# A row-wise tail written out by hand: the last twelve rows of a triangle-multiplication and gated-pair kernel

## The chip, the cores and the metric

The kernel runs on one core of one Trainium2 chip. A core has five engines with instruction queues of their own: TensorE (PE in the profile; its weight loads are PEld), VectorE (DVE), ScalarE (ACT), GpSimd (POOL) and SyncE (SP), which here only issues DMA transfers. Each engine works its queue off in order; an instruction that waits holds up everything behind it. SBUF is the on-chip memory, PSUM the small memory that TensorE writes to and that VectorE and ScalarE can read and write. The metric is the device time of the whole kernel in microseconds (us), as a median over runs.

## The reference

The input is one map x of 384 x 384 positions with 128 channels, in float32. Two layers follow one another.

```
layer 0:  z_n = layernorm(z)                                 # over channels
          a = (z_n Wa + ba) * sigmoid(z_n Wga + bga);  b likewise
          X[i,k,d] = sum_j a[i,j,d] * b[j,k,d]               # per channel a 384x384 product
          pair = z + (layernorm(X) Wo + bo) * sigmoid(z_n Wgo + bgo)
layer 1:  left  = pair W_left + b_left + pair W_eq + b_eq
          gate  = sigmoid(pair W_gate + b_gate)
          right_sum[i] = sum over k of (pair W_right + b_right)
          out   = (left * right_sum * gate) W_out + b_out
          y     = layernorm(out + pair) * ln_scale + ln_bias
```

The last line matters most here: every position's 128 channels get a mean and a variance, are normalised by them, and then scaled and shifted with one value per channel.

## The kernel before

The kernel has three phases. Phase 1 (lines 100 to 388) normalises x, makes the gated factors a and b, and writes them to DRAM with the gate and the residual. Phase 2 (lines 450 to 547) makes the 128 channels' products and their statistics. Phase 3 (lines 552 to 688) finishes layer 0 and does all of layer 1, row by row: row u is one i with its 384 positions, laid out as three pieces (NB = 3) of 128 positions on the 128 partitions, each piece with 128 channels. Rows are loaded and finished in groups of R = 4.

Phase 3 is one software pipeline: the loop over u at line 682 runs through a list of stages, and each stage works on row u minus a lag. The order in which the code names the instructions is the order of every engine's queue. The stages, by function:

- `layer_0` (line 595): three products give the layer-0 output of row u in PSUM; VectorE scales and gates it (L608) and adds the residual (L615) to make `pair`. The same function takes the statistics (L613, L618) of `res` of row u - 8.
- `turn` (line 562): three transposes of `pair` into the PSUM tile `ptr`, of which there is one; ScalarE copies it out to `pairT` and adds up the row for `right_sum` (L568).
- `project` (line 640): the left product (PSUM tile `pleft`, two buffers) and the gate product (PSUM tile `pg`, one buffer); ScalarE's sigmoid (L650). For the first row of a group the right product of the group before is put into the same `pg` bank (L656) and taken out by L652.
- `gate_product` (line 577): VectorE multiplies left and gate to `h` (L580).
- `out_weights` (line 571): ScalarE scales W_out by the row's right sum (L574).
- `layer_1` (line 583): three products of `h` and those weights into the PSUM tile `pf` (two buffers); VectorE adds `pair` and writes `res` to SBUF (L593).
- `norm_factors` (line 620): once per group, on GpSimd: variance plus epsilon, the power -1/2 (L626), mean times that, negated (L625 to L629).
- `normalise` (line 632): ScalarE, in place on `res`, three instructions a row (L635), each with a scale and a bias per partition.
- `store` (line 664): for most groups GpSimd multiplies four rows at once by ln_scale (L674) and adds ln_bias (L675), then SP issues one store of 768 KB (L676). For the last eight rows VectorE does it row by row (L668, L669), with a store of 192 KB each (L670).
- `last_right` (line 658): the right product of the last group.

The loop runs on for 17 steps after the last row has come in, in which fewer and fewer stages have work. In those steps the products, the statistics, the factors and the scaling of rows 372 to 383 follow the same lags as in the loop.

Of the kernel before, what the change touches and what calls it, by code (L numbers as in the profile page):

```python
# [8 lines left out]
FP = mybir.dt.float32  # L9
AF = mybir.ActivationFunctionType  # L10
ALU = mybir.AluOpType
# [4 lines left out]
EPS = 1e-5  # L16
# [3 lines left out]
def kernel(ctx: ExitStack, tc: tile.TileContext, ins, out: bass.AP):  # L20
# [15 lines left out]
    nc = tc.nc  # L36
    ctx.enter_context(tc.manual_schedule())
    P = 128
    x = ins["x"][0]
    N, C = x.shape[1], x.shape[2]  # L40
    NB = N // P
    y_out = out[0]
# [10 lines left out]
    def ctile(shape, name):  # L53
        return const.tile(shape, FP, tag=name, name=name)

    ident = ctile([P, P], "ident")
# [5 lines left out]
    def column(name, q=None):  # L62
        t = ctile([P, 1], "c_" + name)
        (q or nc.sync).dma_start(out=t, in_=ins[name].rearrange("(c o) -> c o", o=1))
        return t

    def rows(name, q=None):
        t = ctile([P, C], "r_" + name)
        (q or nc.sync).dma_start(out=t, in_=ins[name].partition_broadcast(P))
        return t  # L70

    def matrix(name):
        t = ctile([P, P], "m_" + name)
        nc.sync.dma_start(out=t, in_=ins[name])
        return t
# [6 lines left out]
    def over(t, n):  # L82
        return t[:, None, :].to_broadcast([P, n, C])
# [19 lines left out]
    with tc.tile_pool(name="wprep", bufs=6) as wp, tc.tile_pool(name="p1s", bufs=3) as ps, tc.tile_pool(  # L103
        name="p1g", bufs=2
    ) as pgt, tc.tile_pool(name="p1x", bufs=4) as px, tc.tile_pool(name="p1a", bufs=2) as pa_, tc.tile_pool(
        name="p1b", bufs=1, side="right"
    ) as pb_, tc.tile_pool(name="p1t", bufs=2, space=PSUM) as ppt, tc.tile_pool(
        name="p1p", bufs=6, space=PSUM
# [237 lines left out]
        for _ in x_parts:  # L346
# [7 lines left out]
        w_left, w_eq, w_right, w_gate, w_out = (  # L354
            matrix(L1 + k) for k in ("W_left", "W_eq", "W_right", "W_gate", "W_out")
        )
        b_left, b_eq, b_right, b_gate = (column(L1 + k) for k in ("b_left", "b_eq", "b_right", "b_gate"))
        ln_s, ln_b = rows(L1 + "ln_scale"), rows(L1 + "ln_bias")
# [41 lines left out]
    LAST, AHEAD, R, HELD = 8, 6, 4, 16  # L400
    group = {}
# [44 lines left out]
    def advance(g, n=1):  # L446
        for _ in range(n):
            next(g, None)

    with tc.tile_pool(name="p2", bufs=1, side="right", reuse_waits="tile") as p2, tc.tile_pool(  # L450
        name="p2s", bufs=12, side="right", reuse_waits="tile"
    ) as p2s, tc.tile_pool(name="p2p", bufs=5, space=PSUM, reuse_waits="tile") as pp2, tc.tile_pool(
        name="p2q", bufs=2, space=PSUM, reuse_waits="tile"
# [98 lines left out]
    with tc.tile_pool(name="p3s", bufs=4, reuse_waits="tile") as ps, tc.tile_pool(  # L552
        name="p3g", bufs=4, reuse_waits="tile"
    ) as pg3, tc.tile_pool(name="p3y", bufs=2, space=PSUM, reuse_waits="tile") as pyp, tc.tile_pool(
        name="p3p", bufs=1, space=PSUM, reuse_waits="tile"
    ) as pp:
        pairs, hs, wos = {}, {}, {}

        def of(u):
            return group[u // R], u % R  # L560
# [94 lines left out]
        def right(g, pg):  # L655
            nc.tensor.matmul(pg[:, N : N + R], lhsT=w_right, rhs=g["total"], start=True, stop=True)  # L656

        def last_right(u):
            if u == N:
                g, pg = group[N // R - 1], pp.tile([P, 512], FP, tag="pg", name="pg_last")  # L660
                right(g, pg)
                nc.scalar.activation(g["right"], pg[:, N : N + R], AF.Identity, bias=b_right)

        def store(u):
            if u >= N - 2 * R:
                g, i = of(u)
                res = g["res"][:, i]
                nc.vector.tensor_tensor(res, res, over(ln_s, NB), ALU.mult)  # L668
                nc.vector.tensor_tensor(res, res, over(ln_b, NB), ALU.add)  # L669
                nc.sync.dma_start(out=y_out[u].rearrange("(p q) c -> p q c", q=NB), in_=res)  # L670
            elif u % R == 0:
                g = group.pop(u // R)
                res = g["res"].rearrange("p r q c -> p (r q) c")
                nc.gpsimd.tensor_tensor(res, res, over(ln_s, R * NB), ALU.mult)  # L674
                nc.gpsimd.tensor_tensor(res, res, over(ln_b, R * NB), ALU.add)  # L675
                nc.sync.dma_start(out=y_out[u : u + R].rearrange("i (p q) c -> p i q c", q=NB), in_=g["res"])  # L676

        stages = (
            (load, -2 * R), (gate_product, 3), (turn, 2), (out_weights, 7), (layer_1, 8), (layer_0, 0),
            (norm_factors, 12), (normalise, 13), (project, 2), (last_right, 2), (store, 17),  # L680
        )
        for u in range(N + stages[-1][1]):
            for stage, lag in stages:
                if stage is layer_0:
                    stage(u, u - 8)
                elif 0 <= u - lag < N or (stage is last_right and u - lag == N):
                    stage(u - lag)
            advance(behind)


_INS = ["x"] + [
# [33 lines left out]
```

## Time and profile before

| what | us |
|---|---|
| median of three runs | 3340.28 (3338.49 to 3342.46) |
| the profiled execution's own time | 3343.24 |
| its span in the trace | 3341.5 |
| TensorE busy | 3293.7 |
| VectorE busy | 2666.1 |
| ScalarE busy | 2311.3 |
| GpSimd busy | 2091.9 |
| one row in the steady loop of phase 3 (start to start of a row's L593) | 3.0 |
| last row's layer-0 products start | 3304.0 |
| last product of the kernel starts (L592) | 3322.8 |
| VectorE's last instruction ends (L669) | 3338.3 |

The span runs from the first to the last record of one execution; the execution's own time is a little longer. A duration of an instruction is from its start to its end; the next one on the same engine can start up to about 0.1 us before that end, so the distance from start to start is what adds up. "Idle before" names the wait that ended last before an instruction.

### The profile page before, as it was taken

What the parts mean: (1) busy time and instruction counts of PE and PEld (TensorE: products, weight loads), DVE (VectorE), ACT (ScalarE), POOL (GpSimd) and SP (SyncE); (2) the same over time, 40 slices, a digit from 0 to 9 for tenths busy, and PEclk for the clock granted to TensorE, in tenths of its full rate; (3) what the DMA queues carried; (4) which work ended last, traced back from release to release, by engine and by line L of the source; (5) the groups of instructions that cost most, each with busy time, mean ns of one, the idle gap of its engine ahead of it and who ended that gap; (6) DMA issues with size and microseconds to landing.
All of it is one profiled execution on the core that took longest, in us unless ns stands there. A gap on an engine that the chain in (4) does not pass through costs nothing.

```text
span 3341.5 us, 53397 instructions
## 1 busy us (share of the span) xinstructions
PE 3293.7 (99%) x15581; PEld 2191.3 (66%) x15581; DVE 2666.1 (80%) x8599; ACT 2311.3 (69%) x5488; POOL 2091.9 (63%) x1574
## 2 busy tenths in 40 slices
PE   8999999999999999999999999999999999999997
PEld 5555555555555555555555555588888888888885
DVE  8877777777777777455555555799999999999998
ACT  7778787877777788522222222378888888888887
POOL 7555555555555555355555555358888888888887
PEclk9999999999999999999999999999999999999998
DMA  6889899889888889899999999767777777777774
GB/s 226 265 256 273 278 282 282 278 279 281 280 269 264 268 275 282 254 337 318 312 315 311 312 311 304 258 231 262 261 263 262 262 262 264 264 263 263 263 265 142
DMA packets 675522, 910.52 MB, mean 272 GB/s; under 512 B 319520, under 2 KB 616480, under 8 KB 647712
## 3 DMA queue, kind: packets, MB, share of 16 engines
q1 hardware_dynamic: 634192, 680.28, 63.9%
q0 software_dynamic: 40320, 226.51, 19.3%
q8 instruction: 126, 2.06, 0.2%
q14 instruction: 164, 1.34, 0.1%
q10 hardware_dynamic: 720, 0.33, 0.0%
HBM read 454.04 MB, written 452.98 MB: 271 GB/s over the span
## 4 chain that ended last, share of the span: by engine, by line
PE 96%; DVE 2%; POOL 1%; DMA 1%; ACT 0%; issue 0%; POOLq 0%; ACTq 0%; SPq 0%; DVEq 0%
PE pm L488 22%; PE pga L246 8%; PE pa L246 7%; PE pgb L246 7%; PE pb L246 7%; PE py L602 7%; PE pf L592 7%; PE pgo L211 7%; PE pleft L643 7%; PE pg L645 7%; PE ptr L180 4%; PE ptr L566 4%; DMA G<-gt 0%; DVE py L608 0%; PE pg L656 0%
## 5 line engine op out<-in xcount | busy, mean ns | idle before, releaser
L488 PE MATMUL pm<-ab 128*128 128x384 f32 x2304 | 746.6, 487 | 5.8 <-DVE gs L213 5.8
L488 PEld LDWEIGHTS pm<-ab 128*128 128x128 f32 x2304 | 438.9, 191 | 312.4 <-DVE gs L213 6.7
L507 POOL TENSOR_TENSOR acc<-acc,xd 128x384 f32<-128x384 f32 x381 | 380.1, 998 | 362.4 <-DVE xd L500 362.2
L505 ACT ACTIVATE sq<-xd 128x384 f32<-128x384 f32 x381 | 188.5, 495 | 542.3 <-DVE xd L500 542.2
L276 DVE SCALAR_TENSOR_TENSOR bt<-pb,c_L_conv_bb,sgb 128x512 f32<-128x512 f32 x288 | 320.9, 1114 | 243.3 <-ACT zT L191 218.6
L160 ACT ACTIVATE zn<-xt,off,rstd 128x128 f32<-128x128 f32 x1152 | 503.3, 489 | 2.9 <-POOL off L151 2.8
L635 ACT ACTIVATE res<-res,off,rs 128x128 f32<-128x128 f32 x1152 | 482.5, 486 | 18.4 <-POOL off L629 15.7
L500 DVE TENSOR_TENSOR xd<-pm,acc 128x384 f32<-128x384 f32 x381 | 212.2, 557 | 343.3 <-POOL acc L507 321.3
L608 DVE SCALAR_TENSOR_TENSOR py<-py,acc,gr 128x128 f32<-128x128 f32 x1152 | 433.7, 377 | 2.2 <-PE py L602 1.6
L267 POOL DMA_DIRECT2D A<-at x72 | 85.4, 1186 | 539.2 <-DVE at L263 539.2
L251 ACT ACTIVATE sga<-pga,c_L_conv_bga 128x512 f32<-128x512 f32 x288 | 197.9, 687 | 267.6 <-PE pga L246 267.6
L211 PEld LDWEIGHTS pgo<-wT_go,zT 128*128 128x128 f32 x2176 | 285.7, 192 | 130.0 <-issue 66.5
L613 DVE BATCH_NORM_STATS2 st<-res 128x6 f32<-128x128 f32 x1152 | 361.4, 315 | 0.3
L675 POOL TENSOR_TENSOR res<-res,r_L_conv_ln_bias 128x1536 f32<-128x1536 f32 x94 | 324.6, 3453 | 7.4
L171 POOL TENSOR_TENSOR acc<-xt,r_L_conv_b_out 128x2048 f32<-128x2048 f32 x72 | 327.4, 4548 | 1.8
L592 PE MATMUL pf<-w_o,h 128*128 128x128 f32 x2304 | 321.2, 276 | 6.1 <-ACT w_o L574 5.3
L674 POOL TENSOR_TENSOR res<-res,r_L_conv_ln_scale 128x1536 f32<-128x1536 f32 x94 | 325.3, 3461 | 0.2 <-issue 0.2
L650 ACT ACTIVATE sg<-pg,c_L_conv_b_gate 128x384 f32<-128x384 f32 x384 | 223.0, 581 | 144.5 <-PE pg L645 92.6
L602 PE MATMUL py<-w_o,xr 128*128 128x128 f32 x2304 | 321.1, 276 | 0.0
L643 PE MATMUL pleft<-pairT,m_L_conv_W_left 128*128 128x384 f32 x768 | 313.1, 489 | 2.8 <-ACT pairT L568 2.8
L645 PE MATMUL pg<-pairT,m_L_conv_W_gate 128*128 128x384 f32 x768 | 311.1, 487 | 0.0
L141 DVE BATCH_NORM_STATS2 st<-xt 128x6 f32<-128x128 f32 x1152 | 305.5, 265 | 3.7 <-DMA xt<-in_x_dram 3.6
(142 smaller groups left out, 6826.8 us busy)
## 6 DMA issues: line engine op xcount, KB each, us to landing
A<-at POOLq DMA_DIRECT2D x72, 1024.0 KB, 8.5
Z<-acc POOLq DMA_DIRECT2D x72, 1024.0 KB, 8.2
G<-gt POOLq DMA_DIRECT2D x72, 1024.0 KB, 9.2
xr<-X SPq DMA_DIRECT2D x96, 768.0 KB, 6.0
gr<-G SPq DMA_DIRECT2D x96, 768.0 KB, 7.6
zr<-Z SPq DMA_DIRECT2D x96, 768.0 KB, 8.8
X<-xd SPq DMA_DIRECT2D x381, 192.0 KB, 6.2
xt<-in_x_dram SPq DMA_DIRECT2D x71, 1024.0 KB, 17.9
```

Of the source, the lines that this page charges most:

```text
L160: nc.scalar.activation(g["zn"][:, c, :], g["x"][:, c, :], AF.Identity, bias=g["off"][:, c : c + 1], scale=g["rstd"][:, c : c + 1],)
L211: nc.tensor.matmul(pgo[:, c, :], lhsT=zT[:, c, :], rhs=wT["go"], start=True, stop=True)
L246: nc.tensor.matmul(pk, lhsT=wT[k], rhs=zT, start=True, stop=True)
L488: nc.tensor.matmul(products[d, ib], lhsT=ab[:, 0, q, ib * P : (ib + 1) * P], rhs=ab[:, 1, q, :], start=(q == 0), stop=(q == NB - 1),)
L507: nc.gpsimd.tensor_tensor(s1[:, ib, :], s1[:, ib, :], xd, ALU.add)
L592: nc.tensor.matmul(pf[:, q, :], lhsT=h[:, q * P : (q + 1) * P], rhs=w_o, start=True, stop=True)
L602: nc.tensor.matmul(py[:, q, :], lhsT=g["x"][:, i, q * P : (q + 1) * P], rhs=w_o0, start=True, stop=True)
L608: nc.vector.scalar_tensor_tensor(py[:, q, :], py[:, q, :], rs0[:, q, u : u + 1], g["g"][:, i, q, :], ALU.mult, ALU.mult)
L613: nc.vector.bn_stats(b["st"][:, k, q, :], b["res"][:, k, q, :])
L635: nc.scalar.activation(g["res"][:, i, q, :], g["res"][:, i, q, :], AF.Identity, bias=g["off"][:, i, q : q + 1], scale=g["rs"][:, i, q : q ...
L643: nc.tensor.matmul(pleft, lhsT=w_left, rhs=pairT, start=True, stop=True)
L645: nc.tensor.matmul(pg[:, 0:N], lhsT=w_gate, rhs=pairT, start=True, stop=True)
```

## The change

The loop now stops when the last row has come in (u = 383). What was left to the 17 further steps is written out by hand, with D = 384 as the row count. `store` always works on GpSimd and takes the number of rows as an argument. `last_right` is gone; the right product of the last group goes into a bank of the `ptr` tag. Five new functions come in:

- `layer_1_summed`: for rows 382 and 383 the residual is added by TensorE, as a product with the identity into the same bank; there is no VectorE addition, and the sum stays in PSUM.
- `statistics`: the L613 and L618 of a row, by themselves, reading PSUM for those two rows.
- `last_factors`: for the last two groups (376 to 379, 380 to 383) VectorE and ScalarE make the factors instead of GpSimd: ScalarE takes the square root of the variance, VectorE its reciprocal and one Newton step. Each VectorE instruction has at most one tensor operand in SBUF; the rest lies in PSUM, for which two results are copied out to SBUF.
- `normalise_on_gpsimd`: row 376 is normalised by GpSimd with three instructions.
- `normalise_to_bank` and `scale_and_shift`: rows 377 to 383 are normalised by ScalarE into a PSUM bank (the `pleft`, `pf` and `py` tags are used again), and VectorE multiplies in PSUM, adds and writes to SBUF; one store per row.

Rows 372 to 375 keep the factors from GpSimd and are scaled by GpSimd in two halves; row 376 is scaled by GpSimd alone.

```diff
+        def store(u, n=R):
+            if u % n:
+                return
+            g, i = of(u)
+            res = g["res"][:, i : i + n]
+            flat = res.rearrange("p r q c -> p (r q) c")
+            nc.gpsimd.tensor_tensor(flat, flat, over(ln_s, n * NB), ALU.mult)
+            nc.gpsimd.tensor_tensor(flat, flat, over(ln_b, n * NB), ALU.add)
+            nc.sync.dma_start(out=y_out[u : u + n].rearrange("i (p q) c -> p i q c", q=NB), in_=res)
...
-        for u in range(N + stages[-1][1]):
+        for u in range(N):
...
+        def bank(u):
+            tag = {7: "pleft", 6: "pleft", 5: "pleft", 4: "pf", 3: "pf", 2: "py", 1: "py"}[D - u]
+            banks[u] = pyp.tile([P, NB, C], FP, tag=tag, name=f"end_{u}")
+            return banks[u]
+
+        def layer_1_summed(u):
+            pf = bank(u)
+            h, w_o, pair = hs.pop(u), wos.pop(u), pairs.pop(u)
+            for q in range(NB):
+                nc.tensor.matmul(pf[:, q, :], lhsT=ident, rhs=pair[:, q, :], start=True, stop=False)
+                nc.tensor.matmul(pf[:, q, :], lhsT=h[:, q * P : (q + 1) * P], rhs=w_o, start=False, stop=True)
...
+        def last_factors(u):
+            g, _ = of(u)
+            few = pp.tile([P, 4, R, NB], FP, tag="ptr", name=f"few_{u}")
+            v, r, t, rs = (few[:, k] for k in range(4))
+            sd, r_, t_, rs_, off = (
+                pg3.tile([P, R, NB], FP, tag="e" + k, name=f"{k}_{u}", bufs=2) for k in ("sd", "r", "t", "rs", "off")
+            )
+            nc.vector.tensor_scalar(v, g["mv"][:, :, :, 1], EPS, None, ALU.add)
+            nc.scalar.activation(sd, v, AF.Sqrt)
+            yield
+            nc.vector.reciprocal(r, sd)
+            nc.vector.tensor_copy(r_, r)
+            nc.vector.scalar_tensor_tensor(t_, r_, -0.5, r, ALU.mult, ALU.mult)
+            nc.vector.tensor_tensor(t, t_, v, ALU.mult)
+            nc.vector.scalar_tensor_tensor(rs, t, 1.5, r_, ALU.add, ALU.mult)
+            nc.vector.tensor_copy(rs_, rs)
+            nc.vector.scalar_tensor_tensor(off, g["mv"][:, :, :, 0], -1.0, rs, ALU.mult, ALU.mult)
+            g["rs"], g["off"] = rs_, off
+
+        def normalise_on_gpsimd(u):
+            g, i = of(u)
+            for q in range(NB):
+                nc.gpsimd.tensor_scalar(
+                    g["res"][:, i, q, :], g["res"][:, i, q, :], g["rs"][:, i, q : q + 1], g["off"][:, i, q : q + 1],
+                    ALU.mult, ALU.add,
+                )
...
+        def scale_and_shift(u):
+            g, i = of(u)
+            res = g["res"][:, i]
+            nc.vector.tensor_tensor(banks[u], banks[u], over(ln_s, NB), ALU.mult)
+            nc.vector.tensor_tensor(res, banks[u], over(ln_b, NB), ALU.add)
+            nc.sync.dma_start(out=y_out[u].rearrange("(p q) c -> p q c", q=NB), in_=res)
+
+        norm_factors(D - 12)
+        turn(D - 2)
+        gate_product(D - 3)
+        out_weights(D - 7)
+        layer_1(D - 8)
+        statistics(D - 8)
+        turn(D - 1)
+        out_weights(D - 6)
+        project(D - 2)
+        normalise(D - 13)
+        store(D - 16)
+        layer_1(D - 7)
+        statistics(D - 7)
+        gate_product(D - 2)
+        out_weights(D - 5)
...
+        nc.tensor.matmul(pr[:, 0:R], lhsT=w_right, rhs=g["total"], start=True, stop=True)
+        nc.scalar.activation(g["right"], pr[:, 0:R], AF.Identity, bias=b_right)
+        layer_1(D - 6)
+        statistics(D - 6)
+        layer_1(D - 5)
+        out_weights(D - 4)
+        project(D - 1)
+        for u in range(D - 3, D):
+            out_weights(u)
+        statistics(D - 5)
+        gate_product(D - 1)
+        normalise(D - 12)
+        normalise(D - 11)
+        store(D - 12, 2)
+        first = last_factors(D - 8)
+        advance(first)
+        layer_1(D - 4)
+        statistics(D - 4)
+        layer_1(D - 3)
+        advance(first)
+        statistics(D - 3)
+        normalise(D - 10)
+        normalise(D - 9)
+        store(D - 10, 2)
+        layer_1_summed(D - 2)
+        statistics(D - 2)
+        layer_1_summed(D - 1)
+        statistics(D - 1)
+        normalise_to_bank(D - 7)
+        second = last_factors(D - R)
+        advance(second)
+        normalise_on_gpsimd(D - 8)
+        store(D - 8, 1)
+        scale_and_shift(D - 7)
+        advance(second)
+        normalise_to_bank(D - 6)
+        scale_and_shift(D - 6)
+        normalise_to_bank(D - 5)
+        scale_and_shift(D - 5)
+        for u in range(D - R, D):
+            normalise_to_bank(u)
+            scale_and_shift(u)
```

More of the change, by code (lines that the diff above doesn't have):

```diff
@@ L656, in right @@
             nc.tensor.matmul(pg[:, N : N + R], lhsT=w_right, rhs=g["total"], start=True, stop=True)
[L658 to L676, printed above, removed]
+        def store(u, n=R):
[7 more added lines that the diff above has]
+            nc.sync.dma_start(out=y_out[u : u + n].rearrange("i (p q) c -> p i q c", q=NB), in_=res)
         stages = (
             (load, -2 * R), (gate_product, 3), (turn, 2), (out_weights, 7), (layer_1, 8), (layer_0, 0),
-            (norm_factors, 12), (normalise, 13), (project, 2), (last_right, 2), (store, 17),
+            (norm_factors, 12), (normalise, 13), (project, 2), (store, 17),
         )
-        for u in range(N + stages[-1][1]):
+        for u in range(N):
             for stage, lag in stages:
@@ L685 @@
                     stage(u, u - 8)
-                elif 0 <= u - lag < N or (stage is last_right and u - lag == N):
+                elif 0 <= u - lag < N:
                     stage(u - lag)
             advance(behind)
+        D = N
+        banks = {}
+        def bank(u):
[8 more added lines that the diff above has]
+                nc.tensor.matmul(pf[:, q, :], lhsT=h[:, q * P : (q + 1) * P], rhs=w_o, start=False, stop=True)
@@ new lines, in statistics @@
+        def statistics(u):
+            g, i = of(u)
+            for q in range(NB):
+                nc.vector.bn_stats(g["st"][:, i, q, :], banks[u][:, q, :] if u in banks else g["res"][:, i, q, :])
+            for q in range(NB):
+                nc.vector.bn_aggr(g["mv"][:, i, q, :], g["st"][:, i, q, :])
+        def last_factors(u):
[16 more added lines that the diff above has]
+            g["rs"], g["off"] = rs_, off
@@ new lines, in normalise_on_gpsimd, with normalise_to_bank @@
+        def normalise_on_gpsimd(u):
+            g, i = of(u)
+            for q in range(NB):
+                nc.gpsimd.tensor_scalar(
+                    g["res"][:, i, q, :], g["res"][:, i, q, :], g["rs"][:, i, q : q + 1], g["off"][:, i, q : q + 1],
+                    ALU.mult, ALU.add,
+                )
+        def normalise_to_bank(u):
+            g, i = of(u)
+            if u in banks:
+                source = banks[u]
+            else:
+                source = g["res"][:, i]
+                bank(u)
+            for q in range(NB):
+                nc.scalar.activation(
+                    banks[u][:, q, :], source[:, q, :], AF.Identity,
+                    bias=g["off"][:, i, q : q + 1], scale=g["rs"][:, i, q : q + 1],
+                )
@@ new lines, in scale_and_shift @@
+        def scale_and_shift(u):
+            g, i = of(u)
+            res = g["res"][:, i]
[8 more added lines that the diff above has]
+        statistics(D - 8)
@@ new lines @@
+        turn(D - 1)
[7 more added lines that the diff above has]
+        out_weights(D - 5)
+        g = group[D // R - 1]
+        pr = pp.tile([P, N], FP, tag="ptr", name="pr_last")
+        nc.tensor.matmul(pr[:, 0:R], lhsT=w_right, rhs=g["total"], start=True, stop=True)
+        nc.scalar.activation(g["right"], pr[:, 0:R], AF.Identity, bias=b_right)
+        layer_1(D - 6)
```

## The prediction

> **What bounds the kernel now.** I read the page's chain that ended last first, then the engines' busy time in stretches at the end, then the chain inside the last 35 us, then the timeline of single instructions there.
>
> ```profile
> PE 96%; DVE 2%; POOL 1%; DMA 1%; ACT 0%; issue 0%; POOLq 0%; ACTq 0%; SPq 0%; DVEq 0%
> ```
>
> For 96% of the span TensorE carries the chain, and the change touches none of it. The tail is another matter. Columns: stretch, length, busy time of PE, PEld, DVE, ACT and POOL, granted clock, DMA share, GB/s.
>
> ```profile
> 3296.00:3308.00 12.00, 11.77 (x74) 9.31 (x73) 12.00 (x49) 10.56 (x30) 9.88 (x7) 1.00 0.18 66
> 3308.00:3320.00 12.00, 8.19 (x48) 6.07 (x46) 10.51 (x50) 8.82 (x24) 11.59 (x7) 1.00 0.19 68
> 3320.00:3332.36 12.36, 1.65 (x6) 1.35 (x6) 7.77 (x18) 5.02 (x14) 11.75 (x9) 0.51 0.35 127
> 3332.36:3341.50 9.14, 0.00 (x0) 0.00 (x0) 4.47 (x8) 4.73 (x12) 0.00 (x0) 0.50 0.33 121
> ```
>
> From 3308 to 3332 GpSimd is full (11.59 of 12, 11.75 of 12.36) while TensorE empties. The chain says what GpSimd does (start, us):
>
> ```profile
> 3307.57 0.26 POOL rs L625
> ...
> 3310.83 3.42 POOL res L674
> ...
> 3318.18 2.31 POOL rs L626
> ...
> 3328.61 2.57 POOL rs L626
> ...
> 3332.36 0.49 ACT res L635
> ...
> 3337.72 0.56 DVE res L669
> ```
>
> Each group of four rows passes through GpSimd: factors (L625 to L629, 3.2 us, 2.3 of it the power at L626), then two passes over 1536 elements (7.0 us). The last group's factors are ready at 3332.36; four rows at ACT's pace follow (three normalisations of 0.39, 1.17 a row), VectorE ends at 3338.28, the last store issues at 3338.3.
>
> ```profile
> 3325.85 2.57 DVE L668 TENSOR_TENSOR res<-res,r_L_conv_ln_scale 128x384 f32<-128x384 f32 x1
> 3333.65 0.56 DVE L668 TENSOR_TENSOR res<-res,r_L_conv_ln_scale 128x384 f32<-128x384 f32 x1 [1.44 <-ACT res L635]
> out_dram<-res SPq DMA_DIRECT2D x2, 768.0 KB, 3.5
> out_dram<-res SPq DMA_DIRECT2D x8, 192.0 KB, 1.9
> ```
>
> The first two lines are one instruction with GpSimd running and with it idle: 2.57 against 0.56. The last two give landing times: 576 KB more cost 1.6 us, so 0.53 us for 192 KB and 1.37 fixed. The last landing is 3338.3 + 1.9 = 3340.2, and 1.3 us later the span ends.
>
> **What the Trainium skill says.** "SBUF — State Buffer", Who interferes with whom: a VectorE instruction with two SBUF inputs is shut out while a GpSimd instruction reads SBUF. The 2.57 above agrees; L593, with one input in PSUM, keeps 0.52 to 0.56 beside a running L675. "ScalarE: Activation LUTs", What ACT_TABLE_LOAD costs: 1283 ns, plus some 1380 of drain. The trace has 1.28 at L428, but ACT's next instruction starts 0.16 later, so I charge 1.3. "GPSIMD Engine Reference", 3.1 Elementwise: 1.8 cycles an element at best, 2.6 for two inputs. The trace's two-input passes (998 ns for 384, 3453 for 1536) make 2.13 ns an element plus 0.18, which agrees; no row shows 1.8.
>
> **The change part by part.** Up to row 383's layer-0 work the order stays; VectorE reaches the changed part at 3307.35, ACT at 3306.66.
>
> *Removed:* the power chains for rows 376-379 and 380-383 (two of 3.2 us on GpSimd) and the second full pass: store(372)'s 7.0 becomes two halves. *Kept:* the factors of 372-375 (to 3310.83) and store(368).
>
> *ACT.* Rows 382 and 383 are turned back to back: transposes of 383 at 3307.38 (where L643 waited for the same release), then the products of 382 (2 x 0.65) to 3309.27; sigmoid 382 at 3309.32, normalise(371) 3309.79 to 3310.96 (last end 3311.06), out_weights(379), right, out_weights(380) to 3311.9. The product of 379 waits for its weights (3311.40), and project(383) queues behind it: sigmoid 383 at 3313.68, an idle of 1.8. Then 0.47 + 3 x 0.29 weights, six normalisations (2.34) to 3317.46, a table load to 3318.8, root at 3319.0. Sqrt and Identity share a set after it: L568 ran between the Sqrt at L428 and the next load at L650. So one load is new. It lies on VectorE's path.
>
> *VectorE.* Rows 376-381: 1.38 each for add and statistics (L593 starts 3315.94, 3317.35, 3318.72), three gate products at 0.5. From 3307.35: gate product 381 and row 376 to 3309.3, a wait for the product of 377 (behind 382's on PE) to 3309.9, then 377, gate product 382, 378, 379, gate product 383 (4.1 + 1.0) to 3315.05, first v 0.2, row 380 and the addition of 381 (1.95) to 3317.2; it waits for the root until 3319.05 (1.8 lost). The seven small instructions of a factor chain are not in the trace on VectorE with 12 elements. Nearest: 128x1 at 0.14 to 0.16 (L310, L329), gaps of 0.03, reciprocal 2542 ns for 384 = 6.6 an element, so +0.08: 7 x 0.20 + 0.08 = 1.5. Bounds 1.2 (no PSUM charge) and 2.3 (0.33 each, as a 128-wide L608). I take 1.5, twice. Then statistics of 381, 382, 383 at 0.82 (L613 to L618 spacing 0.60 + 0.22): 3320.55 + 2.46 = 3323.0; add 0.25 for the second v; scaling of 377 1.07; second chain 1.5: 3325.85. Six rows remain at 1.07 (L669 to L669: 3328.46, 3329.53, 3330.59), their PSUM operands avoiding the lock: 6.42 + 0.1 gives 3332.4. PSUM-to-PSUM adds 0.03 (L608 against L580) and is inside that. ACT's rows 380-383 start at 3325.9 at 1.17, done 3330.6, ahead of VectorE; row 379's bank waits for 377's scaling (3324.4), no later than needed. By VectorE alone the last landing is 3332.4 + 0.07 + 1.9 = 3334.4.
>
> *GpSimd.* store(368) starts after normalise(371): 3311.12 instead of 3310.79, ends 3318.1. Two-row passes: 0.18 + 768 x 2.13 ns = 1.82, with gap 1.90; four of them: 3318.17 to 3325.69 (372-373 normalised 3317.46, 374-375 by 3321.4, both in time). Then row 376: three tensor_scalar of 128 with two pointer operands. No such row exists. Low: 0.18 + 128 x 1.5 ns (the skill's 1.8 cycles) = 0.37, or 0.25 as L625; high 0.9, twice the two-input price of 0.45. I take 0.45, with gap 3 x 0.53 = 1.6; two passes at 1.08: end 3329.45.
>
> *SP's queue.* This is what decides. store(376) stands ahead of the stores of 377, 378 and 379 on SP, and SP waits for GpSimd. 377 is ready at 3324.4, 378 at 3327.0, 379 at 3328.1: all stay behind 3329.5. Eight stores of 192 KB then leave at the 0.38 us of an issue and are bound by transfer: 3329.5 + 1.37 + 8 x 0.53 = 3335.1, later than VectorE's 3334.4. With the closing 1.3: 3336.4.
>
> *TensorE.* 382 and 383 take six extra identity products; it is idle from 3318.5 before, and they are ready at about 3317, 4 us before VectorE reads them: nothing. Without that cover, 1.7 us each pair of rows. The main loop's store lags the same; no cost.
>
> Sum: 3341.5 - 3336.4 = 5.1 us off the profiled span. The profiled execution took 3343.24, 1.7 over its span and 3.0 over the median of 3340.28; a difference carries over: 3340.28 - 5.1 = **3335.2**, 0.15% less. The runs before spread from 3338.49 to 3342.46, so 0.2%, 6.7 us, is about what a measurement can tell from no change.
>
> **The rivals.**
>
> *1. The unknown prices at their low ends: 3333.5.* tensor_scalar at 0.25 (0.6 off GpSimd's end), store(368) starting at the old 3310.79 because ACT's normalise(371) comes in time (0.3), two-row passes at half of 3.45 with their gap, 1.80 (0.4): GpSimd ends at 3328.15. Transfers at the 389 GB/s that the best slices of the last store traffic show, 0.50 each: last landing 3328.2 + 1.37 + 4.04 = 3333.6. VectorE with factor chains at 1.2 lands at 3333.8, and both end the span at 3335.1: 6.4 saved, 3333.9; if the table load falls into ACT's idle before the last sigmoid's weights, or the last store lands in 1.8 (it did in some), a few tenths more: 3333.5. For: each is a value that some row shows. Against: they must fall low together.
>
> *2. Slower: pointer-scalar tensor_scalar on GpSimd is software-slow.* For: the power takes 2.3 us for 12 elements on the same engine. Against: L625 and L629, plain arithmetic, take 0.25. Row 376 heads SP's queue, so the end moves one for one with three of them. Each of 2.2 us brings no gain (landing 3340.2); each over 4.4 is slower by 0.2%; at 5 us it is 3335.2 + 3 x 4.55 = 3348.9.
>
> *3. The gain is eaten on VectorE: 3339.* PSUM factor chains at the upper 2.3 (+1.6) and PSUM scalings at 1.5 a row instead of 1.07 (+3.0) make VectorE end at 3337.0, landing 3339.0, 1.2 before the old. Against: L593 and L608 show no such price.
>
> **How the numbers follow.** Main case 0.42, own range 3333.4 to 3337.0; the runs' scatter of a microsecond or two puts about a fifth of it beyond 0.2% (0.08). Rival 1 0.40: its time lies on the bound of 3333.6, and since the prices below it are open downwards and those above are the main case, I count four fifths faster (0.32). Rival 2 0.10, slower; rival 3 0.08, same. Faster 0.40, same 0.34 + 0.08 + 0.08 = 0.50, slower 0.10. The range 3331.8 to 3338.6 holds the main case, nearly all of rival 1 and half of rival 3; left out are rival 2, the rest of 3 and rival 1's fastest edge.
>
> **What would show it.** GpSimd's last instruction near 3329.5 and VectorE's near 3332.4; a table load at about 3317.5 with VectorE idle 1.8 us before the first reciprocal; store(376) issued near 3329.5 with three others within 1.5 us behind it; no VectorE scaling over 0.7 us. I am wrong if GpSimd's tensor_scalar leaves 0.25 to 0.9 us, if the load comes in ACT's earlier idle, if SP lets 377 out before 376, or if the rows of the loop before 3307 run at another pace than 3.0 us.

## The result, and the profile after

| | before | changed |
|---|---|---|
| median, us | 3341.02 (3338.49 to 3343.41, 22 runs) | 3335.53 (3333.68 to 3337.78, 22 runs) |
| span of the profiled execution, us | 3341.5 | 3336.0 |
| start of row 383's L615 (the last one) in that span | 3306.67 | 3307.05 |
| from there to the end of the span, "the tail" | 34.83 | 28.95 |

The changed kernel takes 0.9984 of the time of the one before, 95% interval 0.9978 to 0.9989: 5.5 us less. That is faster, by less than the 0.2% that the prediction set as its bound. The tail in the traces is 5.9 us shorter. The tail is the better measure in what follows: over all the profiles here the last L615 starts anywhere from 3302.2 to 3307.1, with the same code ahead of it, so a whole run scatters by some 5 us before the changed part begins. Spans are given to 0.1 us, so a tail is good to about 0.05. Within it the traces repeat closely: in the five kernels whose GpSimd queue is that of the changed kernel (itself, and e7 to e10 below), GpSimd's last instruction ends 22.06 to 22.13 us after that L615.

The page's chain that ended last, of the changed kernel:

```profile
PE 95%; DVE 3%; ACT 1%; DMA 1%; issue 0%; POOL 0%; DVEq 0%; ACTq 0%
```

GpSimd (POOL) is at 0% where it was at 1%; ACT has taken that place. The engines' busy time in the same four stretches (columns: stretch, length, busy time of PE, PEld, DVE, ACT, POOL, granted clock, DMA share, GB/s; 0.38 us later, as row 383 is):

```profile
3296.38:3308.38 12.00, 11.76 (x76) 9.37 (x75) 12.00 (x49) 10.23 (x29) 9.87 (x7) 1.00 0.18 66
3308.38:3320.38 12.00, 9.27 (x64) 7.70 (x62) 9.28 (x45) 9.88 (x26) 11.41 (x7) 1.00 0.16 58
3320.38:3332.74 12.36, 0.00 (x0) 0.00 (x0) 11.34 (x42) 10.20 (x25) 8.54 (x8) 0.63 0.48 176
3332.74:3336.00 3.26, 0.00 (x0) 0.00 (x0) 0.00 (x0) 0.00 (x0) 0.00 (x0) 0.50 0.50 180
```

In the third stretch VectorE goes from 7.77 to 11.34 and ScalarE from 5.02 to 10.20, while GpSimd falls from 11.75 to 8.54. The fourth stretch was 9.14 us long with four rows of work in it; now it is 3.26 us of transfers only. The work that stood behind GpSimd's last factors has moved beside GpSimd's scaling.

The timeline of the changed kernel, single instructions (start, duration, engine, line, then idle before it and the releaser):

```profile
3316.93 0.53 DVE L593 TENSOR_TENSOR res<-pf,pair 128x384 f32<-128x384 f32 x1
3317.74 1.28 ACT L714 ACT_TABLE_LOAD   x1
3319.04 0.18 ACT L714 ACTIVATE sd<-few 128x12 f32<-128x12 f32 x1
3319.25 0.24 DVE L716 RECIPROCAL few<-sd 128x12 f32<-128x12 f32 x1 [1.79 <-ACT sd L714]
3322.00 1.81 POOL L665 TENSOR_TENSOR res<-res,r_L_conv_ln_scale 128x768 f32<-128x768 f32 x1
3323.10 0.56 DVE L749 TENSOR_TENSOR end<-end,r_L_conv_ln_scale 128x384 f32<-128x384 f32 x1
3323.30 5.56 ACT L741 ACTIVATE end<-res,off,rs 128x128 f32<-128x128 f32 x12
3325.68 1.33 POOL L728 TENSOR_SCALAR res<-res,rs,off 128x128 f32<-128x128 f32 x3
3328.17 1.00 POOL L666 TENSOR_TENSOR res<-res,r_L_conv_ln_bias 128x384 f32<-128x384 f32 x1
3328.89 0.57 DVE L749 TENSOR_TENSOR end<-end,r_L_conv_ln_scale 128x384 f32<-128x384 f32 x1 [0.20 <-ACT end L741]
3332.05 0.56 DVE L750 TENSOR_TENSOR res<-end,r_L_conv_ln_bias 128x384 f32<-128x384 f32 x1
```

VectorE waits 1.79 us for the first root, which ScalarE starts 0.01 us after the end of the table load. VectorE's scaling in PSUM starts at 3323.10 in the middle of a GpSimd pass (3322.00 to 3323.81) and still takes 0.56, where the same step took 2.57 before. From 3328.89 on each scaling waits for ScalarE: 0.20 us, then 0.12 twice. GpSimd ends at 3329.17. SP's stores and the transfers (the first two lines are SP's issues, the third the throughput from 3328 to 3336 in 40 slices):

```profile
3329.19 0.34 SPq L667 DMA_DIRECT2D out_dram<-res  x1
3329.64 3.35 SPq L751 DMA_DIRECT2D out_dram<-res  x7
GB/s 0 0 0 0 0 0 0 0 0 0 269 361 376 369 361 377 353 376 361 376 369 338 392 354 369 384 346 376 369 361 376 254 0 0 0 0 0 0 0 0
```

No row of VectorE leaves before 3329.64, though the first, row 377, was finished at 3324.25. It stands behind row 376, which GpSimd ends at 3329.17. The eight stores then run as one block at 340 to 390 GB/s for 4.4 us. The last store is issued near 3332.6, just as VectorE ends (3332.61), and lands (its data is written) 2.2 us later, at 3334.8.

### The profile page after: what moved, and what is told of

Read it like the earlier page. It is cut to its first block, busy times and chain, and to the rows that moved or that the text cites. A ratio compares the mean times of both kernels' runs of the same rounds, so it can differ in the third digit from the quotient of the medians.

```text
span 3336.0 us, 53433 instructions
## 1 busy us (share of the span) xinstructions
PE 3292.2 (99%) x15593; PEld 2191.2 (66%) x15593; DVE 2664.0 (80%) x8611; ACT 2314.1 (69%) x5488; POOL 2089.7 (63%) x1573
## 4 chain that ended last, share of the span: by engine, by line
PE 95%; DVE 3%; ACT 1%; DMA 1%; issue 0%; POOL 0%; DVEq 0%; ACTq 0%
PE pm L488 22%; PE pga L246 8%; PE pa L246 7%; PE pb L246 7%; PE pgb L246 7%; PE pgo L211 7%; PE pf L592 7%; PE py L602 7%; PE pleft L643 7%; PE pg L645 7%; PE ptr L180 4%; PE ptr L566 4%; DVE py L608 1%; DVE st L613 0%; DVE h L580 0%; DMA G<-gt 0%
## 5 line engine op out<-in xcount | busy, mean ns | idle before, releaser
L635 ACT ACTIVATE res<-res,off,rs 128x128 f32<-128x128 f32 x1128 | 472.6, 486 | 7.4 <-POOL off L629 4.8
L608 DVE SCALAR_TENSOR_TENSOR py<-py,acc,gr 128x128 f32<-128x128 f32 x1152 | 387.1, 336 | 2.1 <-PE py L602 1.5
L666 POOL TENSOR_TENSOR res<-res,r_L_conv_ln_bias 128x1536 f32<-128x1536 f32 (+1 forms) x96 | 325.9, 3395 | 7.5
L665 POOL TENSOR_TENSOR res<-res,r_L_conv_ln_scale 128x1536 f32<-128x1536 f32 (+1 forms) x96 | 326.8, 3404 | 0.6 <-ACT res L635 0.3
L613 DVE BATCH_NORM_STATS2 st<-res 128x6 f32<-128x128 f32 x1128 | 309.5, 274 | 0.0
```

Of the source, the lines that this page charges most:

```text
L608: nc.vector.scalar_tensor_tensor(py[:, q, :], py[:, q, :], rs0[:, q, u : u + 1], g["g"][:, i, q, :], ALU.mult, ALU.mult)
L635: nc.scalar.activation(g["res"][:, i, q, :], g["res"][:, i, q, :], AF.Identity, bias=g["off"][:, i, q : q + 1], scale=g["rs"][:, i, q : q ...
```

## The experiments

"Tail" is as in the table above. All ten kernels, with the ratio to the kernel before where there is more than one timed run:

| kernel | tail, us | against changed (28.95) | time, us | ratio to before |
|---|---|---|---|---|
| e1_factors_on_gpsimd | 35.86 | +6.9 | 3341.7 | 1.0002 (0.9994 to 1.0011) |
| e2_only_factors | 30.88 | +1.9 | 3335.88 | 0.9985 (0.9979 to 0.9992) |
| e3_row376_late | 33.40 | +4.45 | 3339.21 | 0.9994 (0.9986 to 1.0003) |
| e4_row376_late_store_last | 29.63 | +0.7 | 3335.08 | 0.9984 (0.9976 to 0.9991) |
| e5_root_first | 29.97 | +1.0 | 3336.21 | 0.9986 (0.9979 to 0.9992) |
| e6_scaling_in_sbuf | 31.41 | +2.5 | 3338.09 | 0.9990 (0.9982 to 0.9999) |
| e7_store376_after_379 | 28.65 | -0.3 | 3334.35 | 0.9981 (0.9973 to 0.9990) |
| e8_idle_filled | 27.31 | -1.6 | 3333.8 | 0.9978 (0.9969 to 0.9987) |
| e9_added_on_vectore | 29.91 | +1.0 | 3335.84 (one run) | |
| e10_banks_in_turn | 27.33 | -1.6 | 3331.68 (one run) | |

**e1_factors_on_gpsimd: the factors alone undone.**

```diff
-        first = last_factors(D - 8)
-        advance(first)
+        norm_factors(D - 8)
...
-        advance(first)
...
-        second = last_factors(D - R)
-        advance(second)
+        norm_factors(D - R)
...
-        advance(second)
```

> The changed kernel with one part undone: the factors of rows 376-379 and 380-383 come from GpSimd's power again, everything else as changed. Theory (GpSimd's queue carries the tail, and the two factor chains taken off it are the gain): GpSimd gets 2 x 3.2 us back; its row 376 ends near 3335.6 in the span instead of 3329.2, eight stores follow, and the span is near 3342.6, 6.6 over the changed kernel and about equal to before (ratio 1.0003). Rival (the new order is the gain, whoever makes the factors): the time stays within 1 us of the changed kernel, 0.998 of before.

The tail is 35.86 against 28.95 and 34.83 of before; the ratio to before is 1.0002. GpSimd's last power and its last pass in this kernel:

```profile
3328.55 2.30 POOL L626 TENSOR_TENSOR rs<-rs,mhalf 128x12 f32<-128x12 f32 x1
3333.93 1.00 POOL L666 TENSOR_TENSOR res<-res,r_L_conv_ln_bias 128x384 f32<-128x384 f32 x1
```

GpSimd ends at 3334.93, 29.0 us after row 383's L615 where it was 22.1, and the tail is longer by the same 6.9. Without the move of the factors the whole gain is gone, and the rest of the change by itself is 1.0 us worse than the old kernel.

**e2_only_factors: the factors alone done**, in the loop of before. `last_factors` is the changed kernel's, without its two pauses.

```diff
         def norm_factors(u):
             if u % R:
                 return
+            if u >= N - 2 * R:
+                last_factors(u)
+                return
             g, _ = of(u)
```

> The kernel before with one part alone: the factors of the last two groups by root and Newton step on ScalarE and VectorE, the old order and the old scaling otherwise. Theory (the factor chains are the gain): GpSimd ends with store(372) near 3326.0; VectorE's first scaling, with two SBUF inputs, waits for that, then eight rows at 1.07 end near 3334.7; span near 3337.9, 3.6 under before (ratio 0.9989), two thirds of the whole change. Rival (the order is the gain): no more than 1 us under before.

The tail is 30.88, 3.95 under before. The timeline of this kernel, GpSimd's last pass and VectorE's first two scalings:

```profile
3318.63 3.43 POOL L696 TENSOR_TENSOR res<-res,r_L_conv_ln_bias 128x1536 f32<-128x1536 f32 x1
3321.79 0.68 DVE L689 TENSOR_TENSOR res<-res,r_L_conv_ln_scale 128x384 f32<-128x384 f32 x1
3322.98 0.55 DVE L689 TENSOR_TENSOR res<-res,r_L_conv_ln_scale 128x384 f32<-128x384 f32 x1
```

GpSimd ends at 3322.06, 19.2 us after row 383's L615 (25.7 in before, with the last factors), and VectorE's eight rows follow unhindered at 1.07. The factor chains alone bring two thirds of the tail's gain (3.95 of 5.88). The order, the sharing of the scaling and the PSUM operands bring the remaining 1.9 on top of them; without them (e1) they cost 1.0. So the parts can't be added up one by one. The medians can't separate this kernel from the whole change (3335.88 and 3335.53); the traces can.

**e3 and e4: row 376 made late, with its store ahead of the others and behind them.** Four further passes put their result aside, so the output is the same.

```diff
             flat = res.rearrange("p r q c -> p (r q) c")
+            if n == 1:
+                for k in range(4):
+                    aside = pg3.tile([P, NB, C], FP, tag="aside", name=f"aside_{k}", bufs=1)
+                    nc.gpsimd.tensor_tensor(aside, flat, over(ln_s, NB), ALU.mult)
```

e4 adds to this, with the store inside `store` kept for n > 1 only:

```diff
         for u in range(D - R, D):
             normalise_to_bank(u)
             scale_and_shift(u)
+        g, i = of(D - 8)
+        nc.sync.dma_start(out=y_out[D - 8].rearrange("(p q) c -> p q c", q=NB), in_=g["res"][:, i])
```

> The changed kernel with four more GpSimd passes over row 376 (results put aside), which make GpSimd's end later by 4 x 1.08 = 4.3 us. Theory A (store(376) heads SP's queue and the finished rows wait behind it): the end moves with it; eight stores leave from 3333.5, last landing 3333.5 + 1.37 + 4.26 = 3339.1, span 3340.4, 4.4 over the changed kernel. Theory B (the end is set by ScalarE's and VectorE's rows alone): only row 376 itself lands late, 3333.5 + 1.9 = 3335.4, span 3336.7, 0.7 over.

> As e3_row376_late, but the store of row 376 is issued after that of row 383. Theory A: nothing waits behind row 376 any more, so of the 4.4 us only row 376's own landing is left: span 3336.7, 0.7 over the changed kernel and 3.7 under e3_row376_late. Theory B: the same time as e3_row376_late.

Tails of 33.40 and 29.63: 4.45 and 0.7 over the changed kernel, as theory A has it, and 3.8 apart for the place of one store. VectorE's last instruction and SP's stores in e3:

```profile
3330.45 0.56 DVE L754 TENSOR_TENSOR res<-end,r_L_conv_ln_bias 128x384 f32<-128x384 f32 x1
3332.33 3.35 SPq L755 DMA_DIRECT2D out_dram<-res  x7
```

and in e4:

```profile
3328.63 0.56 DVE L755 TENSOR_TENSOR res<-end,r_L_conv_ln_bias 128x384 f32<-128x384 f32 x1
3322.77 6.78 SPq L756 DMA_DIRECT2D out_dram<-res  x7
3330.04 0.33 SPq L818 DMA_DIRECT2D out_dram<-res  x1
```

In e3 VectorE is through with all rows at 3331.0 and the first of its stores goes out at 3332.33. In e4 they go out from 3322.77 on, behind the store of rows 374 and 375, and then as they come. SP's order turns a delay of one row on GpSimd into a delay of everything.

**e5_root_first: the wait for the root taken away**, by putting it ahead of the normalisations of rows 372 and 373.

```diff
+        first = last_factors(D - 8)
+        advance(first)
         normalise(D - 12)
         normalise(D - 11)
         store(D - 12, 2)
-        first = last_factors(D - 8)
-        advance(first)
```

> The changed kernel with the first group's root (and its table load) ahead of the normalisations of rows 372 and 373 on ScalarE. VectorE's wait of 1.79 us for the root goes, and store(372) on GpSimd starts 0.8 later (3319.2 instead of 3318.4 in the span). Theory A (GpSimd, SP's queue and the transfers set the end; ScalarE's rows come out the same, since the same work stands ahead of them): the tail, from the start of row 383's L615 to the end of the span, grows from 28.9 to 29.3 to 29.7 us. Theory C (the table load's wait lies on the path, as the prediction had it): the tail shrinks by 1.0 to 1.8, to 27.1 to 27.9.

The tail is 29.97: 1.0 longer, against theory C and 0.3 beyond theory A's range. GpSimd and VectorE in this kernel:

```profile
3317.30 1.80 POOL L665 TENSOR_TENSOR res<-res,r_L_conv_ln_scale 128x768 f32<-128x768 f32 x1 [0.88 <-ACT res L635]
3320.90 0.57 DVE L749 TENSOR_TENSOR end<-end,r_L_conv_ln_scale 128x384 f32<-128x384 f32 x1 [1.58 <-ACT end L741]
3328.57 3.34 SPq L751 DMA_DIRECT2D out_dram<-res  x7
3329.61 0.56 DVE L750 TENSOR_TENSOR res<-end,r_L_conv_ln_bias 128x384 f32<-128x384 f32 x1
```

The wait on VectorE is not gone. It has moved to the scaling of 377, which now waits 1.58 for ScalarE, whose work up to there is the same in another order. And GpSimd has got a wait of 0.88, which it had not. It ends 23.06 us after L615 instead of 22.12, 0.94 later; row 376 and the seven stores behind it follow, and the end of the span moves by 1.02. VectorE itself ends 25.14 us after L615 instead of 25.56, 0.42 earlier, but its rows are held by SP. So of the 1.79 us VectorE gets back only 0.4, because ScalarE, which from the table load on has no idle time left, needs the rest; and even that doesn't reach the end, because the edit also made GpSimd later.

**e6_scaling_in_sbuf: PSUM operands undone for the scaling.**

```diff
-                bank(u)
             for q in range(NB):
                 nc.scalar.activation(
-                    banks[u][:, q, :], source[:, q, :], AF.Identity,
+                    g["res"][:, i, q, :], source[:, q, :], AF.Identity,
...
-            nc.vector.tensor_tensor(banks[u], banks[u], over(ln_s, NB), ALU.mult)
-            nc.vector.tensor_tensor(res, banks[u], over(ln_b, NB), ALU.add)
+            nc.vector.tensor_tensor(res, res, over(ln_s, NB), ALU.mult)
+            nc.vector.tensor_tensor(res, res, over(ln_b, NB), ALU.add)
```

> The changed kernel with one part undone: rows 377 to 383 are normalised into SBUF and scaled there, so both VectorE instructions of a row have two SBUF inputs. Theory (such an instruction is shut out while GpSimd reads SBUF): the scaling of 377 starts beside GpSimd's passes of 1.8 us and takes about that long, GpSimd is pushed back too, VectorE's second factor chain comes 2.5 us later, and the tail is 2.7 to 4 us longer than the 28.9 of the changed kernel. Rival (the place does not matter): ScalarE saves 0.07 on each of its instructions (0.39 to 0.46 apart) and the tail is 0.5 to 1 us shorter.

The tail is 31.41, 2.5 longer, a little under the range given. The scaling of row 377 beside GpSimd's passes:

```profile
3321.42 1.13 DVE L748 TENSOR_TENSOR res<-res,r_L_conv_ln_scale 128x384 f32<-128x384 f32 x1
3321.62 2.41 ACT L740 ACTIVATE res<-res,off,rs 128x128 f32<-128x128 f32 x6
3322.21 2.00 POOL L666 TENSOR_TENSOR res<-res,r_L_conv_ln_bias 128x768 f32<-128x768 f32 x1
3322.58 2.04 DVE L749 TENSOR_TENSOR res<-res,r_L_conv_ln_bias 128x384 f32<-128x384 f32 x1
```

3.2 us for the two instructions that take 1.15 in PSUM, and GpSimd's pass is 0.2 longer too. The rival's part was right by itself: six normalisations in 2.41 are 0.39 apart, and into PSUM they start 0.46 apart on average (twelve in the 5.56 above). It is outweighed.

**e7_store376_after_379: only the order on SP**, the store of 376 moved behind `scale_and_shift(D - 5)`, by the same lines as in e8 below.

> The changed kernel with the store of row 376 issued after that of row 379. Theory A: 377 to 379 leave as they are ready, no burst of eight builds up, and only the last row's own landing is left, 3332.6 + 0.07 + 1.9 instead of 3334.8: the tail is 0.2 to 0.3 us shorter than 28.9. Theory B (ScalarE's and VectorE's rows set the end): the same within 0.1. In the times neither can be seen; the landing of the last store in the trace (2.2 us after its issue before this edit) tells.

The tail is 28.65, 0.3 shorter, in line with theory A. The landing that was to tell agrees: GpSimd and VectorE end as in the changed kernel, 22.1 and 25.6 us after L615, and the last store is issued right behind VectorE in both, but it lands 1.85 us after its issue instead of 2.17. So the block of eight held the end by 0.3 and no more; without a delay on GpSimd the two bounds lie that close together.

**e8_idle_filled: both bounds moved.** As in e4 and e7, the store inside `store` stays for n > 1 only.

```diff
         out_weights(D - 4)
+        normalise(D - 12)
         project(D - 1)
...
-        normalise(D - 12)
-        normalise(D - 11)
-        store(D - 12, 2)
         first = last_factors(D - 8)
         advance(first)
+        normalise(D - 11)
+        store(D - 12, 2)
...
         scale_and_shift(D - 5)
+        g, i = of(D - 8)
+        nc.sync.dma_start(out=y_out[D - 8].rearrange("(p q) c -> p q c", q=NB), in_=g["res"][:, i])
```

> Both bounds moved together: normalise(372) goes into ScalarE's idle 1.7 us ahead of the last sigmoid, the root ahead of normalise(373), and the store of 376 behind that of 379. ScalarE's rows end near 3330.0 instead of 3331.4, VectorE near 3331.1, the last landing near 3333.1 instead of 3334.8: the tail is 1.5 to 1.8 us shorter than the changed kernel's 28.9, near 27.2, and the time 0.9979 of before. If only one bound had moved, the tail would be no more than 0.4 shorter.

The tail is 27.31, 1.64 shorter, and the ratio to before 0.9978. The last sigmoid, the root's chain, the scaling of row 377, SP's last stores and VectorE's last instruction in this kernel:

```profile
3311.19 0.58 ACT L650 ACTIVATE sg<-pg,c_L_conv_b_gate 128x384 f32<-128x384 f32 x1 [0.58 <-PE pg L645]
3314.60 0.22 DVE L717 RECIPROCAL few<-sd 128x12 f32<-128x12 f32 x1
3318.96 0.57 DVE L750 TENSOR_TENSOR end<-end,r_L_conv_ln_scale 128x384 f32<-128x384 f32 x1 [0.42 <-ACT end L742]
3326.43 0.33 SPq L811 DMA_DIRECT2D out_dram<-res  x1
3326.85 1.87 SPq L752 DMA_DIRECT2D out_dram<-res  x4
3327.67 0.56 DVE L751 TENSOR_TENSOR res<-end,r_L_conv_ln_bias 128x384 f32<-128x384 f32 x1
```

ScalarE's idle before that sigmoid is 0.58 instead of 1.73, since row 372 is normalised in it; VectorE no longer waits for the root, and GpSimd has no wait for row 373. e5's edit, which cost 1.0 alone, and e7's, which gained 0.3, are part of a gain of 1.6 once ScalarE's idle is filled; what each of the three gives here was not taken apart. VectorE ends 23.94 us after L615 instead of 25.56. The two SP lines show that row 376 still heads a block: its store goes out at 3326.43 and those of 380 to 383 behind it, though row 380 was ready at 3324.56. With e10 this is the best kernel by tail; by the times its interval overlaps that of the changed kernel.

**e9_added_on_vectore: TensorE's sums undone**, `layer_1` in place of `layer_1_summed` for rows 382 and 383.

> The changed kernel with one part undone: VectorE adds the residual of rows 382 and 383 into SBUF, as for the other rows, instead of TensorE's six identity products. Those two additions stand on VectorE behind its wait for the first root, 0.55 us each. Theory (VectorE from the first root to the second, then ScalarE's rows, make one chain): the second root comes 1.1 later and the tail grows from 28.9 to 29.7 to 30.1 us. Rival (VectorE has room there): the tail stays within 0.2 of 28.9.

The tail is 29.91, 0.96 longer. The second root waits for VectorE 1.52 instead of 0.37:

```profile
3321.39 0.18 ACT L714 ACTIVATE sd<-few 128x12 f32<-128x12 f32 x1 [1.52 <-DVE few L713]
```

So from the first root on, VectorE's instructions are on the path up to the second root, and ScalarE's from there. VectorE ends 1.3 later than in the changed kernel; the tail grows by 0.3 less than that, since the block of eight stores no longer holds the end.

**e10_banks_in_turn: ScalarE's instructions of rows 380 and 381 alternating between two banks**, in e8_idle_filled.

```diff
-        for u in range(D - R, D):
+        bank(D - 4)
+        bank(D - 3)
+        for q in range(NB):
+            for u in (D - 4, D - 3):
+                g, i = of(u)
+                nc.scalar.activation(
+                    banks[u][:, q, :], g["res"][:, i, q, :], AF.Identity,
+                    bias=g["off"][:, i, q : q + 1], scale=g["rs"][:, i, q : q + 1],
+                )
+        scale_and_shift(D - 4)
+        scale_and_shift(D - 3)
+        for u in (D - 2, D - 1):
```

> e8_idle_filled with ScalarE's six instructions of rows 380 and 381 alternating between their two PSUM banks, instead of three into one and then three into the other. In the changed kernel ScalarE's instructions into one bank start 0.46 to 0.49 apart and do not overlap, against 0.39 into SBUF. If the common bank is what keeps them apart, the six now start 0.38 to 0.40 apart and the tail is 0.2 to 0.4 shorter than e8_idle_filled's 27.3. If PSUM as the target is what costs, they stay 0.46 apart and the tail is the same.

The expectation was half right. The alternating instructions (second line) do draw together; the last lines are SP's last stores and VectorE's last instruction:

```profile
3317.21 2.82 ACT L742 ACTIVATE end<-res,off,rs 128x128 f32<-128x128 f32 x6
3319.97 2.37 ACT L817 ACTIVATE end<-res,off,rs 128x128 f32<-128x128 f32 x6
3324.70 0.33 SPq L811 DMA_DIRECT2D out_dram<-res  x1
3325.13 1.88 SPq L752 DMA_DIRECT2D out_dram<-res  x4
3325.78 0.56 DVE L751 TENSOR_TENSOR res<-end,r_L_conv_ln_bias 128x384 f32<-128x384 f32 x1
```

2.37 for six is 0.38 apart, against 0.47 for the six before them. Both rows now become ready only at the end of the six, so VectorE gets little of it: it ends 23.77 us after L615 instead of 23.94 in e8. The tail is 27.33, though, the same as without, and that is SP again: the store of 376 goes out 22.13 us after L615 (22.14 in e8) and the four behind it start at 22.56 in both. What VectorE won, SP's block of stores kept.

## Why the prediction was right

It gave 3335.2 with a chance of 0.5 for a change within 0.2%; 3335.53 was measured, 0.16% under before. Part of that closeness is luck. The saving was put at 5.1 us; it was 5.5 by the medians and 5.9 by the tail. The median of before, 3340.28 from three runs when the prediction was made, is 3341.02 over 22. The larger saving and the higher base nearly cancel. That the change stayed within 0.2% was a near thing as well: the interval, 0.9978 to 0.9989, reaches across it. By the prediction's own steps, with the changed trace's times taken back by the 0.38 us that row 383 comes later there:

| step | predicted | measured |
|---|---|---|
| VectorE through with the addition of 381 | 3317.2 | 3317.08 |
| VectorE's wait for the root | 1.8 | 1.79 |
| a factor chain on VectorE | 1.5 | 1.26 and 1.24 |
| statistics of a row | 0.82 | 0.80 |
| a pass over two rows on GpSimd, start to start | 1.90 | 1.83 (mean of four) |
| three tensor_scalar on GpSimd, up to the next instruction | 1.6 | 1.41 |
| GpSimd's end | 3329.45 | 3328.79 |
| a row of ScalarE's normalisation | 1.17 | 1.38 from SBUF, 1.28 from PSUM |
| VectorE's end | 3332.4 | 3332.23 |
| last landing | 3335.1 | 3334.4 |
| from there to the end of the span | 1.3 | 1.2 |
| shortening of the tail | 5.1 | 5.88 |

*What bounds the tail before* holds: e1 and e2, the factor chain alone undone and alone done, come out at +6.9 and -3.95 where their reckoning from GpSimd's queue gave +6.6 and -3.6.

*SP's queue* holds as a mechanism (e3, e4), and the store block was bound by transfers as computed: 3329.19 + 1.37 + 8 x 0.53 = 3334.8, the landing seen; the eight land 0.51 to 0.54 apart. "This is what decides" holds, but by little: the prediction had VectorE's rows landing 0.7 before the block, and e7 gives 0.3. ScalarE's rows stand just behind.

*Some terms were mis-sized.* GpSimd ends 0.66 earlier than reckoned, most of it from its two-row passes (0.3 over the four) and the three tensor_scalar (0.2). The block of stores follows GpSimd; with the 0.1 less behind the last landing that makes the 0.8 that the tail gained beyond the sum. On VectorE two errors had opposite signs. The factor chains are 0.25 shorter each. ScalarE's normalisation into PSUM takes 1.28 to 1.38 a row, not 1.17 as from SBUF to SBUF, so it and not VectorE's 1.07 paces the last three rows (the waits of 0.20 and 0.12 above). VectorE's earlier start and ScalarE's slower rows nearly cancel in VectorE's end; that 3332.4 came so near was luck too.

*The wait for the root* came exactly, at 1.79. That "it lies on VectorE's path" is worth less than it sounds: e5 takes the wait away, and VectorE's end moves by 0.42, since ScalarE, one step behind, needs the rest. That e5 became slower all the same, by as much as GpSimd became later, fits the prediction's own view that SP's queue behind GpSimd sets the end; theory C in e5's expectation read more into the prediction than it said.

*Rival 1* (all prices low) came true in part: tensor_scalar starts 0.43 to 0.44 apart, the main case's 0.45 without its gap, and the chains are near the low bound of 1.2, while store(368) did wait for normalise(371) as in the main case. *Rival 2* fell: three pointer-scalar instructions on GpSimd take 1.33. *Rival 3* fell for VectorE, whose scalings in PSUM keep 0.56; the extra cost of PSUM turned up on ScalarE, where it was not looked for.

## What to carry to other kernels

When a queue that only issues stores is fed by two engines, put the stores in the order in which their data will be ready: one late producer at the head held seven finished rows here, and 4.4 us of extra lateness on it (e3: GpSimd's end at 26.55 instead of 22.12 us after L615) cost 4.45 at that place and 0.7 at another. Look at that order again after every edit: in e5 and e10 VectorE ended 0.42 and 0.17 earlier, and SP kept both. Before taking away a visible wait, ask which engine one step back needs the same time, and what the edit makes later: a wait of 1.79 us taken away alone gave VectorE 0.42, made GpSimd 0.94 later and the kernel 1.0 us slower; taken away together with the idle time one engine further back it was part of a gain of 1.6. Where the change sits in the last 35 us of a 3.3 ms kernel, measure from a fixed instruction ahead of it to the end of the trace; whole runs scatter by several times the effect of a single edit.

## What the runs showed of the hardware that was not expected

ScalarE's instructions of 128 elements that go into one PSUM bank do not overlap in these kernels: within a row of three from SBUF they start 0.48 to 0.50 us apart, against 0.39 into SBUF, and each starts 0.03 after the end of the one before. The changed kernel's trace tells more: each of these carries a wait for a semaphore (the signal by which instructions wait for each other) that the instruction before it releases, and the ones into SBUF carry no such wait. So the program asks for the wait; whether the bank by itself would keep them apart, no run shows. Alternating between two banks brings them to 0.38 (e10); those carry waits too, which leave no gap. From PSUM into SBUF (e6, rows 382 and 383) six took 2.17, 0.34 apart, the fastest of the four combinations.

A VectorE instruction of 12 elements costs 0.20 to 0.21 us from start to start where each needs the one before, and 0.08 where it doesn't (L721 to L722 at 3320.35 and 3320.43, and on to L702 at 3320.51), with one or two operands in PSUM; the reciprocal of 12 elements adds 0.07.
